# Two third products moved between u and l, and a planner's table of durations set to the trace's, in a two-layer graph kernel

## The chip, the cores and the metric

The kernel runs on one core of one Trainium2 chip. A time is that of the device for one execution, in microseconds (us); the median of several runs is compared. A profiled execution gives a trace besides. T is used below for the time since a pair of batches began on TensorE.

## The reference

The input x is 64 batches of 256 nodes with 512 features in fp32, adj is a 256 x 256 matrix of zeros and ones. Cut to what is computed:

```python
# layer 0
h = relu(layernorm(x))
q, k, v = h @ Wq.T, h @ Wk.T, h @ Wv.T
rel = adj.T * (q @ k.T)                      # per batch, 256 x 256
rel = rel / norm(rel, axis=2)
x = x + rel @ v
# layer 1
h = relu(layernorm(x))
x = x + (adj @ h) @ weight + bias
```

## The kernel before, in words

**Pairs.** Two batches (512 rows) make a pair, and 32 pairs are worked through in one program without a loop at run time; `pairs` writes them all out. Wq and Wk are multiplied once into a matrix m, so that the scores are h m h.

**Three parts.** Every fp32 operand of a matmul is split into u (rounded), l (what is left) and s (a third part that makes up for the cross terms). A product is then three: u by u, l by l, s by s, all summed in one PSUM bank. Between the second and the third, ScalarE multiplies the bank by a number near one (L340). `unit` (L328) writes this down: the matmuls of u and l, `finish`, which writes down the third product of the unit before, then the scaling. So the third product of a unit stands on TensorE after the u and l of the next one, and ScalarE has that long to scale the bank.

**Stages of a pair**, in TensorE's order: g (four units h m, read as gy), v blocks 0 and 1, scores (two units, one for each batch), gather of layer 1 for the pair before (adj times h, four units without a third product), v blocks 2 and 3, mix of the pair before (four units gather times weight, plus bias), attend (four units rel v). Attend's four results are added to x in x_ring, and layer 1's statistics and ReLU follow from them.

**Around them.** ScalarE makes the u of each split out of PSUM (L238, L247), scales banks (L340), does ReLU (L279) and the squares of the scores (L419). VectorE makes s and l (L239, L241; in the gather L248, L249), masks the scores (L415), adds results to x (L496, L555), takes the statistics of the next rows (L265 and L266, four chunks of fresh for layer 0 and four of x_ring for layer 1), and turns 32 x 32 blocks (L301 for h, L461 for the scores). Before each turning, 16 DMAs on SP's queue move the blocks to their places (L293 for h, L455 for the scores). From the turned scores come rel_u (L471, ScalarE), rel_l (L472) and rel_s_parts (L473, both VectorE), from the turned h come h_u (L316), h_l (L318) and hs (L308). SP's queue also loads the next x into fresh and into x_ring (L257), and POOL's stores results (L564).

**The order.** `Plan` (L28) takes every step with its engine, a cost in us, and the names that it reads and writes. `order` (L58) gives each step a due time, counted back from TensorE's ideal sequence, and then plays the engines forward: at each moment the engine that can start first takes, of its steps that are ready, the one that is due first (L91). A step is ready when those that it depends on are over, plus SYNC = 0.12 us if they ran on another engine (L97). The instructions are then issued in the order of these start times, engine by engine, and the scheduler leaves that order as it is. TensorE's own order is that in which the steps are written down. Where ReLU of the next h rows stands, when its block moves start and where VectorE's statistics fall is thus set by the costs in the plan.

Of the kernel before, what the change touches and what calls it, by code (L numbers as in the profile page):

```python
# [27 lines left out]
class Plan:  # L28


    SYNC = 0.12
# [26 lines left out]
    def order(self):  # L58
        ops = self.ops
        at, ideal = 0.0, {}  # L60
        for n, (engine, cost, *_) in enumerate(ops):
            if engine == "PE":
                ideal[n] = at
                at += cost
        due = [ideal.get(n, at + 50.0) for n in range(len(ops))]
        for n in range(len(ops) - 1, -1, -1):
            engine, cost, _, before, _, early = ops[n]
            due[n] -= early
            for m in before:
                e, c, _, _, late, _ = ops[m]  # L70
                due[m] = min(due[m], due[n] - c - late - (self.SYNC if e != engine else 0.0))
        left = [len(op[3]) for op in ops]
        after = [[] for _ in ops]
        for n, op in enumerate(ops):
            for m in op[3]:
                after[m].append(n)
        ready = {}
        when = [0.0] * len(ops)
        for n, k in enumerate(left):
            if not k:  # L80
                ready.setdefault(ops[n][0], []).append(n)
        free, start = {}, [0.0] * len(ops)
        for _ in ops:
            best = None
            for engine, waiting in ready.items():
                if waiting:
                    t = max(free.get(engine, 0.0), min(when[n] for n in waiting))
                    if best is None or t < best[0]:
                        best = t, engine
            t, engine = best  # L90
            n = min((n for n in ready[engine] if when[n] <= t + 0.01), key=lambda n: (due[n], n))  # L91
            ready[engine].remove(n)
            _, cost, _, _, lands, _ = ops[n]
            start[n], free[engine] = t, t + cost
            for m in after[n]:
                same = ops[m][0] == engine and not lands
                when[m] = max(when[m], t + cost + lands + (0.0 if same else self.SYNC))  # L97
                left[m] -= 1
                if not left[m]:
                    ready.setdefault(ops[m][0], []).append(m)  # L100
        self.ends = max(free.values()), at
        return [ops[n][2] for n in sorted(range(len(ops)), key=lambda n: (start[n], n))]
# [11 lines left out]
def kernel(  # L114
# [115 lines left out]
    MM, HALF = 0.231, 0.1185  # L230
# [3 lines left out]
    def split_right_ps(plan, ps, key, parts, names, at, cost=0.49):  # L234
        key = key if isinstance(key, list) else [key]
        u, l, s = ((lambda p=p: p(at)) for p in parts)
        ku, kl, ks = names
        plan.add("ACT", cost, lambda: A.activation(u(), ps, AF.Copy, scale=NEAR), key, ku)  # L238
        plan.add("DVE", 0.63, lambda: V.scalar_tensor_tensor(  # L239
            s(), f(u()), ONE, ps, op0=ALU.mult, op1=ALU.subtract), [*key, *ku], ks)  # L240
        plan.add("DVE", 0.6, lambda: V.scalar_tensor_tensor(  # L241
            l(), f(s()), -CROSS, f(u()), op0=ALU.mult, op1=ALU.add), [*ku, *ks], kl)

    def split_left_ps(plan, ps, key, parts, names, at):
        u, l, s = (p(at) for p in parts)
        ku, kl, ks = names
        plan.add("ACT", 0.49, lambda: A.activation(u, ps, AF.Copy, scale=NEAR), [key], ku)  # L247
        plan.add("DVE", 0.6, lambda: V.tensor_sub(l, ps, f(u)), [key, *ku], kl)  # L248
        plan.add("DVE", 0.6, lambda: V.scalar_tensor_tensor(  # L249
            s, f(l), CROSS + 1.0, ps, op0=ALU.mult, op1=ALU.subtract), [key, *kl], ks)  # L250
# [3 lines left out]
    def load(plan, i, src=None, name="fresh"):  # L254

        dst = fresh if name == "fresh" else ring[i % 2]
        plan.add("SP", 0.65, lambda: SP.dma_start(out=dst, in_=xs[i]), [], keys(name, TC), lands=5.5)  # L257

    def norm(plan, i, layer, src, name):

        st, mv, rs, nb = stats[layer][i % 2]
        k = f"n{layer}{i % 2}"
        for c in range(TC):
            def chunk(c=c):
                V.bn_stats(st[:, c, :], src[:, c, :])  # L265
                V.bn_aggr(mv[:, c, :], st[:, c, :])  # L266
            plan.add("DVE", 0.84, chunk, [(name, c)], [(k, c)])
        every = keys(k, TC)
        plan.add("DVE", 0.12, lambda: V.tensor_scalar(
            rs, mv[:, :, 1], 0.0, EPS, op0=ALU.max, op1=ALU.add), every, [(k, "rs")])  # L270
        plan.add("ACT", 0.2, lambda: A.activation(rs, rs, AF.Sqrt), [], [(k, "rs")])

        def end():
            V.reciprocal(rs, rs)
            V.scalar_tensor_tensor(nb, mv[:, :, 0], -1.0, rs, op0=ALU.mult, op1=ALU.mult)
        plan.add("DVE", 0.25, end, every, [(k, "rs")])

        def relu(dst, c):
            A.activation(dst, src[:, c, :], AF.Relu, bias=nb[:, c : c + 1], scale=rs[:, c : c + 1])  # L279
        return relu, [(k, "rs")]  # L280

    def h_rows(plan, i, src=fresh, name="fresh"):
        relu, needs = norm(plan, i, 0, src, name)
        for c in range(TC):
            plan.add("ACT", 0.72, lambda c=c: relu(h_rel[:, c, :], c),
                     [(name, c), *needs], [("h_rel", c)])
# [10 lines left out]
    def h_turn(plan):  # L297
        def turn(k):
            ht[k] = room(f"ht{k}", 2, T, tag=f"h_s{k}")
            for d in range(2):  # L300
                V.transpose(ht[k][:, d].rearrange("p (c n) -> p c n", c=TC), blocks[:, :, 2 * k + d])  # L301
        for k in range(2):
            plan.add("DVE", 1.16, lambda k=k: turn(k), placed_all, [("h_s", 2 * k), ("h_s", 2 * k + 1)])
# [6 lines left out]
    def h_parts(plan):  # L310
        u, l = h
        for k in range(2):
# [5 lines left out]
            plan.add("DVE", 1.14, lambda k=k, at=at: V.tensor_sub(  # L318
                l[:, at], ht[k], f(u[:, at])), [*ks, *ku], kl)
            plan.add("DVE", 1.14, lambda k=k: h_third(k), [*ku, *kl], ks)  # L320
# [7 lines left out]
    def unit(plan, first, second, drain, on=None):  # L328
# [3 lines left out]
        if on is not None:  # L332
            plan.add("ACT", 0.58, lambda: A.copy(ps, on), ["bias"], [key])
        for cost, fn, reads in first(ps):
            plan.add("PE", cost, fn, reads, [key])
# [4 lines left out]
        plan.add("ACT", 0.49, lambda: A.activation(ps, ps, AF.Copy, scale=ONE), [], [key])  # L340
# [63 lines left out]
    def scores(plan, i):  # L404
        rn = norms[i % 2]
        for b in range(NB):
# [7 lines left out]
            def drain(ps, key, b=b):  # L414
                plan.add("DVE", 0.6, lambda: V.tensor_mul(  # L415
                    rel[:, b].rearrange("p k m -> p (k m)"), ps, f(adjt[0]).rearrange("p k m -> p (k m)")),
                    [key, "adjt"], [("h_rel", b)])
                for k in range(NC):
                    plan.add("ACT", 0.53, lambda k=k: A.activation(  # L419
                        ps[:, ts(k, N)], rel[:, b, k], AF.Square, accum_out=rn[:, b, k : k + 1]),  # L420
                        [("h_rel", b)], [key, (f"rn{i % 2}", b, k)])
            unit(plan, first, second, drain)

    def turn_scores(plan, i, by_pe=False):
# [3 lines left out]
        plan.add("DVE", 0.12, lambda: V.reciprocal(rn, rn), [], sums)  # L428
        if by_pe:
            u, l = (part.rearrange("p b t k n -> p b (t k n)") for part in rel_p)  # L430
            for b in range(NB):
# [11 lines left out]
                plan.add("ACT", 0.49, lambda ps=ps, b=b: A.activation(  # L443
                    u[:, b], ps, AF.Copy, scale=NEAR), [key], [("rel_u", b)])
                plan.add("DVE", 0.63, lambda ps=ps, b=b: V.tensor_sub(
                    l[:, b], ps, f(u[:, b])), [key, ("rel_u", b)], [("rel_l", b)])
                plan.add("DVE", 0.6, third, [("rel_u", b), ("rel_l", b)],
# [11 lines left out]
        for b in range(NB):  # L459
            for k in range(NC):  # L460
                plan.add("DVE", 0.33, lambda b=b, k=k: V.transpose(  # L461
# [10 lines left out]
        plan.add("DVE", 1.14, lambda: V.tensor_sub(l, flat_raw(), f(u)), [*halves, *rel_u], rel_l)  # L472
        plan.add("DVE", 1.14, lambda: V.scalar_tensor_tensor(  # L473
            whole(rel_third()), f(l), CROSS, f(u), op0=ALU.mult, op1=ALU.subtract), [*rel_u, *rel_l], halves)

    def attend(plan, i, exact):
        slot, rn = i % 2, norms[i % 2]
        for c in range(TC):
# [16 lines left out]
            def drain(ps, key, b=b, n=n, c=c):  # L495
                plan.add("DVE", 0.63, lambda: V.scalar_tensor_tensor(  # L496
# [4 lines left out]
            unit(plan, first, second, drain)  # L501

    def layer_1(plan, i, exact):
        slot = i % 2
        relu, needs = norm(plan, i, 1, ring[slot], f"x{slot}")
        for c in range(TC):
            x_c = [(f"x{slot}", c), *needs]
            if not exact:
                plan.add("ACT", 0.72, lambda c=c: relu(changing("late", "h2", 8, D)[:, c], c), x_c,
# [4 lines left out]
            plan.add("ACT", 0.72, lambda c=c: relu(raw()[:, c % 2], c), x_c,  # L514
                     [("raw", 0), ("raw", 1)] if not c else k)
            plan.add("ACT", 0.53, lambda c=c, u=u: A.copy(late(u), raw()[:, c % 2]), k, [("late", u)])
            plan.add("DVE", 0.6, lambda c=c, u=u, l=l: V.tensor_sub(
# [28 lines left out]
    def mix(plan, i, blocks_of=range(4)):  # L546
        slot = i % 2
        for c in blocks_of:
# [5 lines left out]
            def drain(ps, key, c=c):  # L554
                plan.add("DVE", 0.6, lambda: V.tensor_add(  # L555
# [63 lines left out]
    adjt = []  # L619
# [4 lines left out]
    def first_turn(plan):  # L624

        u, l = h
        for d in range(DC):
# [6 lines left out]
            plan.add("ACT", 0.49, lambda ps=ps, d=d: A.activation(  # L634
                u[:, d], ps, AF.Copy, scale=NEAR), [key], [("h_u", d)])
            plan.add("DVE", 0.63, lambda ps=ps, d=d: V.tensor_sub(
                l[:, d], ps, f(u[:, d])), [key, ("h_u", d)], [("h_l", d)])
        for k in range(2):
            kept = [(f"h_{q}", d) for q in "ul" for d in (2 * k, 2 * k + 1)]
            plan.add("DVE", 1.14, lambda k=k: h_third(k), kept, [("h_s", 2 * k), ("h_s", 2 * k + 1)])  # L640
# [7 lines left out]
    def first_g(plan):  # L648

        banks = [next_bank() for _ in range(DC)]  # L650
        for k in range(3):
            for e, (ps, key) in enumerate(banks):
# [3 lines left out]
                if k == 2:  # L656
                    plan.add("ACT", 0.49, lambda ps=ps: A.activation(ps, ps, AF.Copy, scale=ONE), [], [key])
# [21 lines left out]
    def pairs(exact):  # L679
# [6 lines left out]
        plan.add("ACT", 0.49, lambda: A.copy(adjt[0].rearrange("p m n -> p (m n)"), bank[6]), [("bank", 6)], ["adjt"])  # L686
# [83 lines left out]
```

## Time and profile before

| | |
|---|---|
| median of 3 runs | 1571.62 us (1569.84 to 1572.21) |
| profiled execution | 1571.74 us |
| its span, first to last instruction | 1569.96 us |
| VectorE busy | 1357.6 us, 86% |
| ScalarE busy | 1023.8 us, 65% |
| scaling of banks, L340 | 572 times, 583 ns each |
| load of fresh, issue to landing | 5.9 us |
| load of x_ring, issue to landing | 7.9 us |
| row moves of h (L293), 64 KB each | 496, 2.1 us to landing |
| block moves of the scores (L455), 32 KB each | 464, 1.9 us to landing |

The page gives busy times with the tail of each instruction; on VectorE an operation of 128 x 512 is listed with some 0.68 us, and the next starts 0.60 us after it. A matmul of 512 columns is listed with 389 ns, while four of them start within 0.907 us, since they overlap. PEld is the load of a weight, which runs ahead of its matmul. In a list of waits, the engine to the left of the arrow waited for the one to the right; in a timeline the wait stands in brackets behind the instruction that it delayed. SPq is SP's queue of DMA issues.

### The profile page before, as it was taken

What the parts mean: (1) busy time and instruction counts of PE and PEld (TensorE: products, weight loads), DVE (VectorE), ACT (ScalarE), POOL (GpSimd) and SP (SyncE); (2) the same over time, 40 slices, a digit from 0 to 9 for tenths busy, and PEclk for the clock granted to TensorE, in tenths of its full rate; (3) what the DMA queues carried; (4) which work ended last, traced back from release to release, by engine and by line L of the source; (5) the groups of instructions that cost most, each with busy time, mean ns of one, the idle gap of its engine ahead of it and who ended that gap; (6) DMA issues with size and microseconds to landing.
All of it is one profiled execution on the core that took longest, in us unless ns stands there. A gap on an engine that the chain in (4) does not pass through costs nothing.

```text
span 1570.0 us, 22385 instructions
## 1 busy us (share of the span) xinstructions
PE 1557.2 (99%) x8046; PEld 1322.8 (84%) x8046; DVE 1357.6 (86%) x2419; ACT 1023.8 (65%) x1941; POOL 24.3 (2%) x39
## 2 busy tenths in 40 slices
PE   9999999999999999999999999999999999999998
PEld 6788888888888888888888888888888888888886
DVE  6997889898888988898888889888989888988786
ACT  5567666676667676666666676766666766767654
POOL 0000000000000000000000000000000000000000
PEclk9999999999999999999999999999999999999999
DMA  6431444324444334443244442344433344433311
GB/s 195 113 81 41 118 111 120 69 77 111 115 115 93 82 81 120 110 119 68 77 112 114 114 112 67 81 118 111 118 75 85 97 119 110 121 67 79 84 54 56
DMA packets 433127, 153.62 MB, mean 98 GB/s; under 512 B 389872, under 2 KB 390128, under 8 KB 433008
## 3 DMA queue, kind: packets, MB, share of 16 engines
q1 hardware_dynamic: 422784, 116.46, 31.5%
q0 software_dynamic: 8432, 32.51, 5.6%
q10 hardware_dynamic: 1792, 3.15, 0.5%
q8 instruction: 65, 1.06, 0.3%
q14 instruction: 54, 0.44, 0.1%
HBM read 70.78 MB, written 33.55 MB: 66 GB/s over the span
## 4 chain that ended last, share of the span: by engine, by line
PE 83%; SPq 5%; DVE 5%; DMA 4%; ACT 2%; issue 1%; ACTq 0%; DVEq 0%
PE bank L228 83%; SPq L293 4%; DMA fresh<-in_x_dram 2%; SPq L455 2%; ACT h_rel L279 1%; DVE st L265 1%; DMA bias_bc<-in_L_gnn_bias_dram 1%; DMA x_ring<-in_x_dram 1%; DMA h_rel<-h_rel 0%; DVE gy_s L239 0%; DVE gy_l L241 0%; ACT bank L340 0%; DVE h_rel L415 0%; DVE late_parts L239 0%; DVE mv L266 0%
## 5 line engine op out<-in xcount | busy, mean ns | idle before, releaser
L340 ACT ACTIVATE bank<-bank 128x512 f32<-128x512 f32 x572 | 333.4, 583 | 321.5 <-PE bank L228 318.3
L228 PE MATMUL bank<-wv_s,hs 128*128 128x512 f32 x512 | 139.9, 395 | 0.2
L228 PE MATMUL bank<-w_u,gy_u 128*128 128x512 f32 x512 | 137.9, 391 | 0.0
L228 PE MATMUL bank<-wv_u,h_u 128*128 128x512 f32 x512 | 137.6, 390 | 0.0
L228 PE MATMUL bank<-w_s,gy_s 128*128 128x512 f32 x512 | 137.5, 391 | 0.0
L228 PE MATMUL bank<-w_l,gy_l 128*128 128x512 f32 x512 | 137.3, 390 | 0.0
L228 PE MATMUL bank<-wv_l,h_l 128*128 128x512 f32 x512 | 136.9, 389 | 0.0
L228 PE MATMUL bank<-h_u,m_u 128*128 128x512 f32 x512 | 136.5, 389 | 0.3 <-DVE m_s L239 0.3
L228 PE MATMUL bank<-h_l,m_l 128*128 128x512 f32 x512 | 136.6, 389 | 0.1
L228 PE MATMUL bank<-hs,m_s 128*128 128x512 f32 x512 | 136.3, 389 | 0.0
L239 DVE SCALAR_TENSOR_TENSOR gy_s<-gy_u,bank 128x512 fp32r<-128x512 f32 x128 | 86.2, 676 | 43.3 <-ACT gy_u L238 43.3
L228 PEld LDWEIGHTS bank<-w_u,gy_u 128*128 128x128 f32 x512 | 96.0, 188 | 20.8
L228 PEld LDWEIGHTS bank<-w_s,gy_s 128*128 128x128 f32 x512 | 95.7, 188 | 21.2 <-ACT bank L340 1.2
L228 PEld LDWEIGHTS bank<-w_l,gy_l 128*128 128x128 f32 x512 | 96.1, 188 | 20.7
L228 PEld LDWEIGHTS bank<-h_u,m_u 128*128 128x128 f32 x512 | 96.0, 188 | 20.5 <-ACT wv_u L238 0.5
L228 PEld LDWEIGHTS bank<-h_l,m_l 128*128 128x128 f32 x512 | 96.0, 188 | 20.4 <-DVE h_l L318 0.5
L228 PEld LDWEIGHTS bank<-wv_l,h_l 128*128 128x128 f32 x512 | 96.1, 188 | 20.2
L228 PEld LDWEIGHTS bank<-hs,m_s 128*128 128x128 f32 x512 | 96.1, 188 | 19.9
L228 PE MATMUL bank<-adjt_r,late_parts 128*128 128x256 f32 x896 | 112.8, 277 | 0.0
L228 PEld LDWEIGHTS bank<-wv_s,hs 128*128 128x128 f32 x512 | 92.8, 188 | 22.8 <-ACT bank L340 5.2
L228 PEld LDWEIGHTS bank<-wv_u,h_u 128*128 128x128 f32 x512 | 93.7, 188 | 17.8
L228 PEld LDWEIGHTS bank<-adjt_r,late_parts 128*128 128x128 f32 x896 | 107.5, 188 | 0.0
(110 smaller groups left out, 3078.3 us busy)
## 6 DMA issues: line engine op xcount, KB each, us to landing
fresh<-in_x_dram SPq DMA_DIRECT2D x31, 1024.0 KB, 5.9
blocks<-h_rel SPq DMA_DIRECT2D x496, 64.0 KB, 2.1
x_ring<-in_x_dram SPq DMA_DIRECT2D x31, 1024.0 KB, 7.9
out_dram<-x_ring POOLq DMA_DIRECT2D x31, 1024.0 KB, 5.3
h_rel<-h_rel SPq DMA_DIRECT2D x464, 32.0 KB, 1.9
blocks<-in_L_gnn_Wv_dram ACTq DMA_DIRECT2D x1, 1024.0 KB, 10.9
x_ring<-in_L_gnn_weight_dram SPq DMA_DIRECT2D x1, 1024.0 KB, 12.4
out_dram<-x_ring SPq DMA_DIRECT2D x4, 256.0 KB, 2.3
```

Source lines behind the costliest of these rows:

```text
L228: nc.tensor.matmul(out, left, right, start=first, stop=True, skip_group_check=True)
L239: plan.add("DVE", 0.63, lambda: V.scalar_tensor_tensor(s(), f(u()), ONE, ps, op0=ALU.mult, op1=ALU.subtract), [*key, *ku], ks)
L265: V.bn_stats(st[:, c, :], src[:, c, :])
L279: A.activation(dst, src[:, c, :], AF.Relu, bias=nb[:, c : c + 1], scale=rs[:, c : c + 1])
L293: plan.add("SP", 0.65, lambda j=j, k=k: SP.dma_start(out=blocks[ts(j, S), :, :, ts(k, S)], in_=hv[ts(k, S), :, :, ts(j, S)]), keys("h_rel" ...
L340: plan.add("ACT", 0.49, lambda: A.activation(ps, ps, AF.Copy, scale=ONE), [], [key])
L455: plan.add("SP", 0.65, lambda j=j, k=k: SP.dma_start(out=pv[ts(j, S), :, ts(k, S)], in_=rv[ts(k, S), :, ts(j, S)]), [("h_rel", 0), ("h_rel ...
```

## The change

It has two parts, and adds or removes no instruction.

First, `unit` gets a parameter `behind`: the number of the step of u and l ahead of which the waiting third product is written down. Two places use it. In scores, batch 0, the third product of v block 1 comes after the u matmuls and ahead of the l matmuls. In attend, block 0, the third product of the unit before (mix block 3) comes between u and l. All other units keep their order.

Second, the plan's costs are set to durations of the trace, each changed by some hundredths of a us (the largest: the turning of h, L301, from 1.16 to 1.24, ReLU from 0.72 to 0.76, L274 and L275 together from 0.25 to 0.37, the landing of fresh from 5.5 to 6.0 and of x_ring from 5.5 to 8.0), and a step on VectorE that depends on another one on VectorE is ready only CHAIN = 0.11 us after it, where it was ready at once.

The diff, cut to its core (the other changed lines only change a cost in the same way):

```diff
-    SYNC = 0.12
+    SYNC, CHAIN = 0.12, 0.11
...
-                when[m] = max(when[m], t + cost + lands + (0.0 if same else self.SYNC))
+                when[m] = max(when[m], t + cost + lands + (self.CHAIN * (engine == "DVE") if same else self.SYNC))
...
-    MM, HALF = 0.231, 0.1185
+    MM, HALF = 0.229, 0.1165
...
-        plan.add("DVE", 0.63, lambda: V.scalar_tensor_tensor(
+        plan.add("DVE", 0.61, lambda: V.scalar_tensor_tensor(
             s(), f(u()), ONE, ps, op0=ALU.mult, op1=ALU.subtract), [*key, *ku], ks)
...
-        plan.add("SP", 0.65, lambda: SP.dma_start(out=dst, in_=xs[i]), [], keys(name, TC), lands=5.5)
+        plan.add("SP", 0.65, lambda: SP.dma_start(out=dst, in_=xs[i]), [], keys(name, TC), lands=6.0 if name == "fresh" else 8.0)
...
-            plan.add("DVE", 0.84, chunk, [(name, c)], [(k, c)])
+            plan.add("DVE", 0.82, chunk, [(name, c)], [(k, c)])
...
-        plan.add("DVE", 0.25, end, every, [(k, "rs")])
+        plan.add("DVE", 0.37, end, every, [(k, "rs")])
...
-            plan.add("DVE", 1.16, lambda k=k: turn(k), placed_all, [("h_s", 2 * k), ("h_s", 2 * k + 1)])
+            plan.add("DVE", 1.24, lambda k=k: turn(k), placed_all, [("h_s", 2 * k), ("h_s", 2 * k + 1)])
...
-    def unit(plan, first, second, drain, on=None):
+    def unit(plan, first, second, drain, on=None, behind=9):
...
-        for cost, fn, reads in first(ps):
+        for n, (cost, fn, reads) in enumerate(first(ps)):
+            if n == behind:
+                finish(plan)
             plan.add("PE", cost, fn, reads, [key])
         finish(plan)
...
-            unit(plan, first, second, drain)
+            unit(plan, first, second, drain, behind=9 if b else 2)
...
-            unit(plan, first, second, drain)
+            unit(plan, first, second, drain, behind=9 if c else 1)
```

## The prediction

> **What bounds the kernel now.** I read the page's busy shares first, then the waits of all engines, then the chain that ended last, then the timelines of two pairs of batches.
>
> ```profile
> PE 1557.2 (99%) x8046; PEld 1322.8 (84%) x8046; DVE 1357.6 (86%) x2419; ACT 1023.8 (65%) x1941; POOL 24.3 (2%) x39
> ```
>
> TensorE is busy 99% of the span, with no order of work that could shorten its matmuls; only its gaps can be won or lost. I took the start of the first h_u,m_u matmul of each pair from the timeline of TensorE and subtracted neighbours. Thirteen of the pairs 2 to 30 take 47.54 us (two of them 47.55), the rest up to 48.61. So 47.54 is the floor of a pair, and the excess over it, summed over these 29 pairs, is 6.95 us. That sum, about 3 us at the start (pairs 0 and 1) and 1.3 us in pair 31 are all there is to win by reordering.
>
> The chain that ended last says where the excess comes from:
>
> ```profile
> 737.50 1.35 SPq L293
> 738.90 1.76 SPq L293
> 741.39 1.39 SPq L293
> 744.17 5.73 DMA fresh<-in_x_dram
> ...
> 801.60 721.01 PE bank L228 x3766
> ```
>
> Row moves of h (L293), then the load of fresh behind them, and then a stall; after 801.6 us TensorE alone is the chain. The timelines of VectorE and TensorE show such a stall:
>
> ```profile
> 798.54 0.69 DVE L265 BATCH_NORM_STATS2 st<-fresh 128x6 f32<-128x512 f32 x1 [0.72 <-DMA fresh<-in_x_dram]
> 800.16 0.65 DVE L239 SCALAR_TENSOR_TENSOR gy_s<-gy_u,bank 128x512 fp32r<-128x512 f32 x1
> 800.85 0.69 DVE L241 SCALAR_TENSOR_TENSOR gy_l<-gy_s,gy_u 128x512 fp32r<-128x512 f32 x1
> 801.60 0.50 PE L228 MATMUL bank<-h_l,gy_l 128*128 128x256 f32 x2 [0.34 <-DVE gy_l L241]
> ```
>
> The statistics of fresh stand in VectorE's queue ahead of the last gy_l. When the load is late, gy_l is late, and TensorE waits. The waits list this load 19 times, 13.8 us. The shifted ScalarE work behind it explains the later small waits on the bank scaling of L340.
>
> **What the Trainium skill says.** "TensorE: Matmul & The Clock Gate", Back-to-back issue gap, gives N/2.4 + 2.5 ns, 216 ns for N = 512; here four matmuls start 0.907 us apart, 227 ns each, so the floor is near it. "VectorE: DVE Perf Modes", The DRAIN you can't avoid, says a semaphore between chained operations costs nothing extra. The trace differs, and decides: L239 to L241, which depends on it, starts 0.71 us later, independent neighbours 0.60. The change's new delay of 0.11 is thus true of this trace. "DMA: Bandwidth & Descriptors", Anatomy of one DMA, puts some 2.0 us of fixed cost on a DMA; the 32 KB moves of L455 land after 1.9.
>
> **The change, part by part.** Times below are T, counted from the start of a pair; the floor pair that begins at 1308.89 us gives them. Its lines:
>
> ```profile
> 1332.53 0.69 DVE L415 TENSOR_TENSOR h_rel<-bank,adjt_r 128x512 f32<-128x512 f32 x1 [1.25 <-PE bank L228]
> ...
> 1347.69 1.20 DVE L318 TENSOR_TENSOR h_l<-ht,h_u 128x1024 fp32r<-128x1024 f32 x1
> 1348.81 1.21 DVE L472 TENSOR_TENSOR rel_l<-rel_s_raw,rel_u 128x1024 fp32r<-128x1024 f32 x1
> 1350.06 1.23 DVE L473 SCALAR_TENSOR_TENSOR rel_s_parts<-rel_l,rel_u 128x1024 fp32r<-128x1024 f32 x1
> 1351.20 1.22 DVE L318 TENSOR_TENSOR h_l<-ht,h_u 128x1024 fp32r<-128x1024 f32 x1
> ```
>
> ```profile
> 1350.97 0.39 PE L228 MATMUL bank<-v_low,rel_l 128*128 128x512 f32 x1
> 1351.20 0.39 PE L228 MATMUL bank<-late_parts,rel_l 128*128 128x512 f32 x1
> 1351.43 1.08 PE L228 MATMUL bank<-w_s,gy_s 128*128 128x512 f32 x4
> 1353.25 0.39 PE L228 MATMUL bank<-v_low,rel_s_parts 128*128 128x512 f32 x1
> ```
>
> *The moved third products.* No instruction is added. In scores, four wv_s matmuls (0.91 us) go ahead of h_l,gy_l; in attend, four w_s matmuls go ahead of the first rel_l. So gy_l is due 0.91 us later, and rel_l at T = 42.08 + 0.91 = 42.99. The scaling of the moved bank (L340, 0.58 us) loses that much cover: for mix block 3 its product now starts at 42.09; its last matmul ends at 40.88, and 0.04 + 0.58 + 0.05 later it is scaled, 41.55. Cover 0.5 us: nothing lost. Attend block 0 is worse: its last rel_l matmul would start at 43.22 and end 0.39 later; scaling ends at 44.23, plus 0.05. Its third product is due at 44.37. A late weight load costs more than its lateness: a matmul whose load had to wait keeps the next one off for 0.335 us instead of 0.227, so I add 0.108. 44.28 + 0.108 - 44.37 = 0.02 us. Nothing, so long as ScalarE is free; the built order puts no other ScalarE work between those scalings any more.
>
> *The new order.* Listing the instructions of both kernels engine by engine, I find that VectorE's order changes in every pair. The statistics of fresh leave the place ahead of gy_l: three of four chunks now stand among the gathers' splits, and ReLU, row moves and the load of fresh follow 10 us later than before. ReLU ends about T = 8.5 or 9.4; sixteen moves took 10.8 us where no output store ran (pairs 0 and 1), 12.2 to 14.1 otherwise; the store is over at about T = 6 now, so I take 10.8; 5.9 us of landing gives T = 25.2 or 26.1. The first statistics come at 27.7 or 28.6. The wait on fresh is gone, and with it the waits on gy_l and their wake: I credit 6.3 of the 6.95 us, and leave 0.65 for waits on L455 (pairs 2, 22, 23).
>
> *What it costs.* Three chunks at 0.81 us are 2.44 us put between the second L415 (T = 23.64) and L473. Before, VectorE idled there: 0.3 us ahead of L248, 0.7 after L428, 0.3 ahead of L301. And the delay of 0.11 lets the planner fill it: L473 depends on L472, isn't ready when L472 ends, and another ready operation of 0.58 or 1.14 us is put between. From pair 2 two orders alternate, 14 times each.
> Even pairs: L415 at 23.64, first L248 at 24.25; then fourteen operations at 0.60 (8.4), three chunks (2.44), four L301 (2.45), four L461 (1.31), L555 0.58, L318 1.13, L428 0.1, one dependent step 0.11: L472 at 40.75. L318 follows, then L473 at 43.02; it takes 1.23, release 0.05, load 0.108: 44.41 against 44.37, 0.04 us of wait.
> Odd pairs: the first L248 comes ahead of the second L415, at 23.27; the same sum with 0.6 for L415, 0.27 us of wait for ScalarE (L238) and both L318 ahead gives L472 at 41.69. rel_l is good at 43.06 against 42.99 (0.07). L555 is next, and L473 at 43.41 gives 44.80 against 44.44: 0.36. Together 0.43 us.
> 14 x 0.04 + 14 x 0.43 = 6.6 us. Each start may be off by 0.2 us, so 2 to 13 us; I take 6.6.
>
> *Start and end.* At the start the four chunks of fresh go into VectorE's idle time, seen here:
>
> ```profile
> 21.65 0.69 DVE L636 TENSOR_TENSOR h_l<-bank,h_u 128x512 fp32r<-128x512 f32 x1 [3.46 <-ACT h_u L634]
> ```
>
> The h_l behind are done 1.6 us sooner, but L274 still waits for ScalarE's root at 24.9, so the first L239 of m starts at 25.4, not 25.99: 0.6 us won. In pair 0 rel_l follows w_l without L274, L275 and L428 ahead: 0.5 us. In pair 31, 0.2. Pair 1 I count at nothing.
>
> *The sum.* The profiled execution took 1571.74 us (span 1569.96), 0.12 above the median of 1571.62. 1571.74 + 6.6 - 6.3 - 0.6 - 0.5 - 0.2 = 1570.7 us: no change that counts.
>
> **Rivals.** *The chain is on time* (1564.1): all credits, no new wait. L473 need only start 0.04 us sooner in even and 0.43 in odd pairs. For it: the ends of the matmuls are modelled, and 0.108 may not apply. Against: VectorE runs without a gap from L248 on, at spacings that repeat to 0.01 us between floor pairs.
> *The load of fresh is late again*, slower: if sixteen moves keep taking 13.3 us, the load lands at 9.4 + 13.3 + 5.9 = 28.6, and odd pairs want it at 27.7; 0.9 us x 14 = 12.6 more, 1583.3. It decides from 11.9 us of moves on. Against it: the store no longer runs beside them. For it: the loads now share the DMA engines with L455.
> *VectorE's chain is later than I count*, 0.25 us in all 28 pairs: 1577.7.
> That nothing is reordered is ruled out by the listing.
>
> **How the numbers follow.** Forecast 0.42, on time 0.29, late load 0.20, later chain 0.09. About 0.2% (3.1 us) is what a measurement of this kernel can tell from no change. On time is nearly all faster, and the low side of the forecast adds some: 0.34. The late load, the later chain and a little of the forecast are slower: 0.30. Same 0.36. The range, 1563.5 to 1581, leaves out the low end of the first rival and the high end of the late load.
>
> **What would show it.** Pair starts: even pairs 47.6, odd 48.0, hardly any spread. VectorE's wait on fresh near 0. Waits of TensorE on rel_s_parts (L473), none on gy_l. If L265 waits on fresh at T = 28, or TensorE's floor changes, I am wrong.

## The result and the profile after

The changed kernel takes 1575.01 us (median; 1573.49 to 1576.78), the kernel before, beside it on the same chip, 1571.65 us (1569.84 to 1574.32): a ratio of 1.0020, 95% interval 1.0014 to 1.0026. It is slower by 0.2%, where I had expected 1570.7 us. The profiled execution took 1576.78 us, with a span of 1574.35 us, 4.4 us more than before. It is the slowest of the 22, 1.8 us above their median, so a part of the loss in its trace belongs to this execution alone. Numbers of lines from L343 on are those of before plus 3: L415 is now L418, L455 is L458, L472 is L475, L473 is L476.

Cut by the start of each pair on TensorE, as in the prediction, the two spans differ like this (us):

| | before | after | difference | predicted |
|---|---|---|---|---|
| up to the start of pair 0 | 26.81 | 26.40 | -0.4 | -0.6 |
| pair 0 | 36.89 | 35.86 | -1.0 | -0.5 |
| pair 1 | 49.75 | 48.94 | -0.8 | 0 |
| pairs 2 to 30, above 29 x 47.54 | 6.94 | 14.57 | +7.6 | +0.3 |
| pair 31 and the end | 70.90 | 69.93 | -1.0 | -0.2 |

The loss is all in the steady pairs. Two lines of the page answer to those of before, the busy times and the chain that ended last:

```profile
PE 1557.1 (99%) x8046; PEld 1318.6 (84%) x8046; DVE 1331.0 (85%) x2419; ACT 1024.9 (65%) x1941; POOL 24.3 (2%) x39
...
PE 72%; DVE 14%; SPq 7%; ACT 2%; DMA 2%; issue 1%; DVEq 0%; ACTq 0%
```

TensorE does the same work, and VectorE is less busy than before (1331.0 us for 1357.6), but it now lies on the chain with 14% of the span, for 5% before. The waits of all engines tell which of its operations are late (engine and line, the releaser; us in total, times, the longest):

```profile
PEld bank L228 <- ACT bank L343: 17.6, 38, 1.6
DVE h_rel L418 <- DMA blocks<-h_rel: 11.6, 5, 2.5
...
PEld bank L228 <- DVE rel_l L475: 6.2, 15, 0.9
...
PE bank L228 <- DVE rel_s_parts L476: 2.9, 15, 0.5
DVE st L265 <- DMA fresh<-in_x_dram: 2.3, 1, 2.3
...
DVE rel_s_raw L464 <- DMA h_rel<-h_rel: 1.9, 3, 1.0
```

The wait on fresh, 13.8 us in 19 places before, is down to one of 2.3, and TensorE waits on gy_l no more. In their place stand rel_l and rel_s_parts, 15 times each, about once in each odd pair, as predicted. Of the first line, 8.5 us before, 14.1 us are the weight load of the first rel_s_parts product, once in each pair: with the moved products it follows close on the scaling of its bank. TensorE itself waits 1.1 us in all on the scaling. (In odd pairs the line names the wrong engine: in pair 13 the scaling is over at T = 44.25, and that load starts at 44.67, as rel_s_parts is done.) New, and in no part of my sum, is the second line: the masking of the scores (L418), which writes into h_rel, waits for the row moves of h, which read h_rel.

An undisturbed odd pair (pair 13, from 639.08) shows the predicted wait. First VectorE, then TensorE (start, duration; the wait in brackets):

```profile
678.46 2.32 DVE L318 TENSOR_TENSOR h_l<-ht,h_u 128x1024 fp32r<-128x1024 f32 x2
680.69 1.22 DVE L475 TENSOR_TENSOR rel_l<-rel_s_raw,rel_u 128x1024 fp32r<-128x1024 f32 x1
681.82 0.68 DVE L558 TENSOR_TENSOR x_ring<-bank,x_ring 128x512 f32<-128x512 f32 x1
682.43 1.22 DVE L476 SCALAR_TENSOR_TENSOR rel_s_parts<-rel_l,rel_u 128x1024 fp32r<-128x1024 f32 x1
```

```profile
683.23 0.39 PE L228 MATMUL bank<-late_parts,rel_l 128*128 128x512 f32 x1
683.79 0.47 PE L228 MATMUL bank<-v_low,rel_s_parts 128*128 128x512 f32 x1 [0.17 <-DVE rel_s_parts L476]
```

L558 stands between L475 and L476. L476 starts at T = 43.35 (predicted 43.41), and the matmul that reads it starts 0.56 us after its neighbour, not 0.23. Such pairs take 47.98 us; undisturbed even pairs 47.57. That is 0.44 and 0.03 above 47.54, 14 of each: 6.6 us, as in the sum. But in 16 of the 29 pairs there is more: eight odd pairs (3, 5, 7, 17, 19, 21, 25, 27) are together 4.3 us above 47.98, and the even ones 3.7 us above 47.57. These 8.0 us are what the experiments had to explain.

### The profile page after: what moved, and what is told of

The parts are those of the page before. It is cut to its first block, busy times and chain, and to the rows that moved or that the text cites. A ratio compares the mean times of both kernels' runs of the same rounds, so it can differ in the third digit from the quotient of the medians.

```text
span 1574.4 us, 22399 instructions
## 1 busy us (share of the span) xinstructions
PE 1557.1 (99%) x8046; PEld 1318.6 (84%) x8046; DVE 1331.0 (85%) x2419; ACT 1024.9 (65%) x1941; POOL 24.3 (2%) x39
## 4 chain that ended last, share of the span: by engine, by line
PE 72%; DVE 14%; SPq 7%; ACT 2%; DMA 2%; issue 1%; DVEq 0%; ACTq 0%
PE bank L228 72%; SPq L458 5%; DVE h_l L318 2%; SPq L293 2%; DVE rel_s_raw L464 1%; DVE x_ring L558 1%; DVE rel_s_parts L476 1%; DVE rel_l L475 1%; DVE ht L301 1%; DMA h_rel<-h_rel 1%; DVE late_parts L241 1%; DVE gy_s L249 1%; DVE late_parts L239 1%; DVE gy_l L248 1%; DVE st L265 1%
## 5 line engine op out<-in xcount | busy, mean ns | idle before, releaser
L343 ACT ACTIVATE bank<-bank 128x512 f32<-128x512 f32 x572 | 333.3, 583 | 371.1 <-PE bank L228 369.9
L418 DVE TENSOR_TENSOR h_rel<-bank,adjt_r 128x512 f32<-128x512 f32 x64 | 44.1, 689 | 95.0 <-PE bank L228 65.4
L228 PEld LDWEIGHTS bank<-w_u,gy_u 128*128 128x128 f32 x512 | 96.0, 188 | 20.8
L228 PEld LDWEIGHTS bank<-wv_l,h_l 128*128 128x128 f32 x512 | 96.1, 188 | 20.1
```

The source lines that it names most:

```text
L228: nc.tensor.matmul(out, left, right, start=first, stop=True, skip_group_check=True)
L343: plan.add("ACT", 0.5, lambda: A.activation(ps, ps, AF.Copy, scale=ONE), [], [key])
L418: plan.add("DVE", 0.605, lambda: V.tensor_mul(rel[:, b].rearrange("p k m -> p (k m)"), ps, f(adjt[0]).rearrange("p k m -> p (k m)")), [key ...
```

## The experiments

All were run in five rounds beside the kernel before; ratios are to that one, since the same kernel before had medians from 1572.07 to 1575.33 us in these jobs. "Excess" is the sum of pairs 2 to 30 above 29 x 47.54 us in the profiled execution. That is one execution of each kernel: those of the changed kernel and of experiment 4 were the slowest of their kernels' runs, that of experiment 5 was the fastest, so differences of 1 to 2 us between two excesses show little. The recorded expectations call the runs by names: e2_costs is experiment 2 here, e3_nochain 3, e6_ahead 7, e9_e3pool 9 and e13 or e13_chainonly 11.

**1. Moved products alone.** The kernel before with the new `unit` and nothing else:

```diff
+            if n == behind:
+                finish(plan)
```

> The kernel before with the moved third products alone (all costs as before, no delay). VectorE and ScalarE keep the order of before, only TensorE's order changes. Theory (the move is harmless or helps, the new order of VectorE is what costs): the 1.8 us of waits on gy_l go, the bank scalings of attend block 0 cost 0.02 us a pair; 1569.5 us, 0.1 to 0.2% under before. Rival (the moved third product takes the cover of its bank scaling and is itself the loss): a wait on the scaling of 0.2 us or more in every attend, 1577 us or more.

Measured 1574.67 us, ratio 1.0007 (0.9999 to 1.0016): no change that this measurement can tell, with an excess of 10.25 us. Neither number came true. Undisturbed pairs are at 47.57. Where the moves of the scores land late, as in pair 22, the moved product has lost the cover that it had. Here is that pair on ScalarE and TensorE in the kernel before, and then with the moved products:

```profile
1112.48 0.58 ACT L340 ACTIVATE bank<-bank 128x512 f32<-128x512 f32 x1
...
1113.15 1.14 PE L228 MATMUL bank<-w_s,gy_s 128*128 128x512 f32 x4
```

```profile
1111.35 1.04 ACT L473 ACTIVATE rel_u<-rel_s_raw 128x1024 fp32r<-128x1024 f32 x1
1112.30 1.51 ACT L279 ACTIVATE h_rel<-fresh,nb,rs 128x512 f32<-128x512 f32 x2
1113.71 0.57 ACT L342 ACTIVATE bank<-bank 128x512 f32<-128x512 f32 x1
...
1114.33 1.18 PE L228 MATMUL bank<-w_s,gy_s 128*128 128x512 f32 x4 [0.63 <-ACT bank L342]
```

ScalarE does rel_u and two ReLU ahead of the bank's scaling, all delayed by those moves. Before, the scaled bank was ready (1113.06) as its product's turn came (1113.15). Now the turn comes 0.91 us sooner, and TensorE waits 0.63. The pair is 48.48 us instead of 47.61.

**2. The new model alone.** The changed kernel with the third products at their old places:

```diff
-            unit(plan, first, second, drain, behind=9 if b else 2)
+            unit(plan, first, second, drain)
...
-            unit(plan, first, second, drain, behind=9 if c else 1)
+            unit(plan, first, second, drain)
```

> The changed kernel with its costs and its delay, but with no third product moved. Theory (rel_l and rel_s_parts late on VectorE): rel_l is due 0.91 us earlier than in the changed kernel, so odd pairs wait 0.98 us for rel_l where they wait 0.43 in all now; 14 x 0.55 = 7.7 us more than the changed kernel, some 1583 us. Rival (the moved products are the loss): at or under the kernel before, 1570 us.

Measured 1583.63 us, ratio 1.0063 (1.0050 to 1.0077), as the theory had it. Undisturbed odd pairs take 48.47 us, even ones 47.54. So the model's order costs 0.93 us in an odd pair, of which the moved products take back 0.49 by making rel_l due later. The two parts of the change are not a sum: alone the products bring nothing, with the new order 0.4%.

**3. Without the delay.**

```diff
-    SYNC, CHAIN = 0.12, 0.11
+    SYNC, CHAIN = 0.12, 0.0
```

> The changed kernel with CHAIN = 0: moved products and costs of the trace, but no delay between dependent VectorE steps. The built order has no statistics of fresh among the gathers' splits, rel_s_parts stands right behind rel_l, and the row moves are early again as in the kernel before. Theory (the delay brought the bad order): no wait on rel_s_parts, waits on fresh shorter than before; 1568 us. Rival (the durations brought it): as the changed kernel, 1575 us.

Measured 1571.8 us, ratio 0.9986 (0.9980 to 0.9993): faster than both kernels. Its order is again that of the kernel before round rel_l, ReLU and row moves lie round the start of the pair, all pairs have a floor of 47.61, and the wait on fresh is back (14.3 us). So without the delay the slowdown is gone.

**4. rel_l and rel_s_parts as one step**, so that nothing can be put between them:

```diff
-        plan.add("DVE", 1.135, lambda: V.tensor_sub(l, flat_raw(), f(u)), [*halves, *rel_u], rel_l)
-        plan.add("DVE", 1.135, lambda: V.scalar_tensor_tensor(
-            whole(rel_third()), f(l), CROSS, f(u), op0=ALU.mult, op1=ALU.subtract), [*rel_u, *rel_l], halves)
+        def both():
+            V.tensor_sub(l, flat_raw(), f(u))
+            V.scalar_tensor_tensor(
+                whole(rel_third()), f(l), CROSS, f(u), op0=ALU.mult, op1=ALU.subtract)
+        plan.add("DVE", 2.38, both, [*rel_u], [*rel_l, *halves])
```

> The changed kernel with rel_l and rel_s_parts written down as one step of the plan (2.38 us on VectorE), so that nothing stands between them; nothing else is edited. Theory (the filler between them is the steady loss): odd pairs keep 0.07 us of wait on rel_l, 0.36 on rel_s_parts goes, even pairs lose their 0.03; 14 x 0.39 = 5.5 us less than the changed kernel, 1569.5 us. Rival (the loss is in the disturbed pairs, whose row moves or loads are late): no more than 1 us less, 1574 us.

Measured 1577.04 us, ratio 1.0016 (1.0008 to 1.0024), a miss. What it was made for did come: undisturbed pairs take 47.60 in both parities, so the 0.44 us of an odd pair were the operation between the two. But the order of even pairs changed too. The first chunk of fresh is now the second operation after the masking instead of the eighth, and the load isn't there:

```profile
DVE st L265 <- DMA fresh<-in_x_dram: 16.5, 15, 2.9
```

The even pairs' excess went from 4.11 to 10.45 us, more than the odd ones gained (10.46 to 6.93). (The medians of the two kernels do not differ clearly.) This is the prediction's rival of the late load, by another door: the moves are no slower, but the statistics are asked for sooner.

**5. Scores in a tile of their own.** The order on TensorE, VectorE and ScalarE stays that of the changed kernel; only the write after read on h_rel goes. (Lines are one higher.)

```diff
-    wq_last, wk_last = room("wq_last", D), room("wk_last", D)
+    rel_own = room("rel_own", T * NC)
+    wq_last, wk_last = rel_own[:, :D], rel_own[:, D:]
...
-    rel = flat_rel[:, : T * NC].rearrange("p (b k m) -> p b k m", b=NB, k=NC)
+    rel = rel_own.rearrange("p (b k m) -> p b k m", b=NB, k=NC)
```

> The changed kernel in its own order, but the masked scores get a tile of their own instead of the first half of h_rel (the room comes from two weight tiles that only the start uses). So L418 no longer has to wait until the sixteen row moves have read h_rel. Theory: this write-after-read is what delays the disturbed odd pairs (3, 5, 7, 17, 19, 21, 25, 27: together 4.3 us above the 47.98 of the clean ones). It goes: odd pairs all near 48.0, no wait of L418 on the moves, ratio to the kernel before 0.9995 (1.0021 less 4.3 of 1575). Clean even and odd pairs stay at 47.57 and 47.98. Rival: something else makes the disturbed pairs late (the moves themselves, or the loads beside them), and the ratio stays at 1.002.

Measured 1575.81 us, ratio 1.0006 (0.9998 to 1.0014), between the two theories. Pair 21 in the changed kernel, SyncE's queue and VectorE, and then the same pair with the own tile:

```profile
1031.72 11.55 SPq L293 DMA_DIRECT2D blocks<-h_rel  x16
...
1045.28 0.69 DVE L418 TENSOR_TENSOR h_rel<-bank,adjt_r 128x512 f32<-128x512 f32 x1 [2.98 <-PE bank L228]
```

```profile
1031.93 11.16 SPq L294 DMA_DIRECT2D blocks<-h_rel  x16
...
1044.47 0.69 DVE L419 TENSOR_TENSOR rel_own<-bank,adjt_r 128x512 f32<-128x512 f32 x1 [1.96 <-PE bank L229]
```

In the first, the last of sixteen moves is issued at T = 20.15 and lands 2.1 us later, at T = 22.26; L418 starts at T = 22.79 instead of the 21.76 of undisturbed pairs. In each pair of the changed kernel in which L418 is late, it starts 0.2 to 0.5 us after the last landing. The brackets name TensorE in both, although it was long done in the first: the instruction waits for several things. In the second the moves are late too (the last lands at T = 21.85), and L419 starts at T = 21.77, in this pair and in every other from pair 2 on, also where the last move lands at T = 23.06 (pair 27). So the lateness of L418 is the write after read, and with it go seven of the eight odd pairs, 4.1 of the 4.3 us; in pair 17 L418 is only 0.33 us late, and the moves of the scores are late too. But the odd pairs as a whole gained nothing: their excess is 10.80 us for 10.46, since each now pays a new wait:

```profile
DVE ht L302 <- DMA h_rel<-rel_own: 2.1, 11, 0.2
```

The wait on the moves has gone over to their next reader, the turning of h, which had needed none as long as L418 ahead of it had waited. There it costs 0.27 us: L302 starts at T = 34.16 in 13 of the 14 odd pairs, instead of 33.89 in undisturbed ones, though the row moves are over by T = 23.1. The list names the moves of the scores, which L302 does not read; they signal on the same semaphores. Its start does not follow their landings, so I put the 0.27 us down to the wait itself, which no run tests. In the even pairs an operation of 0.57 us stands right ahead, and L302 starts at T = 34.00 in both kernels. All odd pairs now take 48.27 to 48.37 but for pair 3. What the trace gains in its pairs, it gains in the even ones (excess 2.68 us for 4.11, 0.9 of it in pair 26). The ratios differ by 0.14%, some 2.2 us; with some 4 us of new waits (14 x 0.29) beside it, I estimate that the write after read was worth about 6 us.

**6. Early row moves in the new order.**

```diff
-    def h_place(plan, early=8.0):
+    def h_place(plan, early=14.0):
```

> The changed kernel with the row moves due 14 us ahead of their need in the planner instead of 8: ReLU and moves come at the start of the pair again, no chunk of fresh lies among the splits of the gathers, the load of fresh is again issued behind sixteen early moves. Theory: the loss of the changed kernel comes from the late ReLU and moves, not from the moved products or the model's durations as such. Clean pairs 47.57 in both parities (as its pair 30 shows, which has this order), no wait of L418 on the moves, but the wait on fresh is back at some 14 us, of which about 6 reach TensorE as in the kernel before; ratio 0.9995 to 1.0. Rival: the delay between VectorE operations has spoiled the order elsewhere too, and the ratio stays at 1.002.

Measured 1576.95 us, ratio 1.0016 (1.0008 to 1.0024): the rival's number, by another way. From pair 5 on the theory holds: both parities are at 47.57, and 26 pairs are together 4.3 us above that. But pairs 2, 3 and 4 take 49.28, 52.41 and 50.47 us, 9.5 us more than 47.57 each. Their moves start at T = 3.3 to 4.8, where from pair 5 on they start 5.1 us ahead of the pair; the load stands behind them, and the statistics wait for it up to 5.8 us. It takes this order three pairs to get back into step.

**7. A planner that looks ahead.**

```diff
-            n = min((n for n in ready[engine] if when[n] <= t + 0.01), key=lambda n: (due[n], n))
+            n = min((n for n in ready[engine] if when[n] <= t + 0.12), key=lambda n: (due[n], n))
+            t = max(t, when[n])
```

> The changed kernel with a planner that, at each choice, also takes an operation that becomes ready within 0.12 us if it is due earlier, so that the delay of 0.11 between dependent VectorE operations no longer calls for another operation in between. Theory: the delay is in the durations rightly, and it does harm only because the greedy planner fills each gap of 0.11 with an operation of 0.4 to 0.8 us; with this the order is nearly that without the delay, and so is the time: ratio 0.9985. Rival: the harm comes from the longer due times or from the other durations, and the ratio stays near 1.002.

Measured 1566.44 us, ratio 0.9950 (0.9936 to 0.9964): the fastest beside 8, ahead of both kernels, and better than expected. rel_s_parts follows rel_l again, undisturbed pairs take 47.57, the excess is 5.38 us. The wait on fresh is still there:

```profile
DVE st L266 <- DMA fresh<-in_x_dram: 12.2, 17, 1.4
```

But now most of it is covered. By the trace, the planner has put the masking of the first scores between the two steps of the statistics' end (L269 and L274 of before), where it stood behind both, and so behind ScalarE's root too. No run tests that step alone.

**8. Looking ahead without the delay** (3 and 7 together).

> The changed kernel without the delay (as e3_nochain), but with the planner that looks 0.12 us ahead (as e6_ahead). Theory: without the delay there is no gap of 0.11 to be filled, so looking ahead gives next to nothing here: ratio near that of e3_nochain (0.9986), and the delay with the look ahead (0.995) is better than no delay. Rival: looking ahead is a gain by itself, whatever the delay: ratio 0.995.

Measured 1564.65 us, ratio 0.9956 (0.9943 to 0.9970). My theory for this falls: looking ahead gains by itself, whatever the delay; the two intervals overlap. So experiment 7 does not show that a model with the true delay is worth anything, only that looking ahead undoes its harm. The plan also has SYNC = 0.12 us between engines, and looking ahead covers that too; whether its gain comes from there was not tested.

**9. The load of fresh on GpSimd's queue**, in experiment 3's kernel:

```diff
+        E, q = ("POOL", G) if name == "fresh" else ("SP", SP)
-        plan.add("SP", 0.65, lambda: SP.dma_start(out=dst, in_=xs[i]), [], keys(name, TC), lands=6.0 if name == "fresh" else 8.0)
+        plan.add(E, 0.8 if name == "fresh" else 0.65, lambda: q.dma_start(out=dst, in_=xs[i]), [], keys(name, TC), lands=6.0 if name == "fresh" else 8.0)
```

> The changed kernel without the delay (as e3_nochain), and with the load of fresh issued by GpSimd's queue, so that it is not behind the sixteen row moves on SyncE. Theory: what is left above the clean pairs in the kernel before and in e3_nochain (some 7 us) is the load of fresh that is issued only after 10.8 us of moves. It then starts as soon as the ReLU has read fresh, the wait of the statistics on it (14.3 us in e3_nochain) goes below 3, and the ratio is 0.9945. Rival: the load shares the transfer engines with the moves, or waits behind the store on GpSimd's queue, and what it gains is lost on the moves: ratio 0.9985 as without it.

Measured 1570.82 us, ratio 0.9974 (0.9964 to 0.9984). The wait on fresh fell from 14.3 us to one of 2.2 at the start, and the excess from 9.33 to 6.05 us. Of the 0.41% that I expected over experiment 3, 0.12 came, and the two intervals overlap. The trace shows two reasons. Pairs 13 to 16 and 18 to 20 are still 0.28 to 0.85 us above 47.61; in pair 13 the turning of the scores (L465) starts 0.7 us late and TensorE waits 0.58 us on the scaling, as in experiment 1. And the time from TensorE's last matmul to the end is 7.8 us instead of 5.8.

**10. Both, 7 and 9.**

> The planner of e6_ahead and the load of fresh on GpSimd's queue as in e9_e3pool. Theory: the two gains are of different waits, so they add: the clean pairs stay at 47.57, the wait of the statistics on fresh goes from 12.2 us to below 3, and of it some 3 us had reached TensorE: ratio 0.9935 (e6_ahead has 0.995). Rival: in e6_ahead the wait on fresh was hidden already, and the pairs that are left above the clean ones (12 to 20, in e9_e3pool too) wait for the row moves of the scores: ratio 0.995 as without it.

Measured 1567.93 us, ratio 0.9973 (0.9963 to 0.9983), not better than 7 but rather worse (the intervals just touch). The rival was right that the wait on fresh was covered already: the excess is 5.56 us with it and 5.38 without. The rest is at both ends: pair 0 starts 0.8 us later, and the end takes 8.3 us instead of 6.2.

**11. The delay alone** in the kernel before:

```diff
-                when[m] = max(when[m], t + cost + lands + (0.0 if same else self.SYNC))
+                when[m] = max(when[m], t + cost + lands + (0.11 * (engine == "DVE") if same else self.SYNC))
```

> The kernel before with the delay of 0.11 between dependent VectorE operations in its model, and nothing else of the change. Its built order has ReLU and moves at the start of the pair as before, but two steps of h's low parts ahead of rel_l and the drain of x between rel_l and rel_s_parts. Theory: the delay by itself already brings the worse order round rel_l, and without the moved products that costs as in pair 30 of e2_costs, which has the same steps there: 0.25 us in each of 29 pairs, 7.3 us, ratio 1.0046. Rival: the delay harms only with the other durations, which push the ReLU to the middle of the pair: ratio 1.000.

Measured 1618.04 us, ratio 1.0290 (1.0276 to 1.0304), far off both. The waits say why:

```profile
DVE st L265 <- DMA fresh<-in_x_dram: 60.5, 31, 3.6
PEld bank L228 <- DVE gy_l L241: 31.5, 26, 2.1
PE bank L228 <- DVE gy_l L241: 26.3, 25, 1.9
```

The gaps of 0.11 us are now filled with the chunks of fresh, between the splits that TensorE waits for, and ahead of the landing.

**12. The same order with the load on GpSimd's queue** (the planner still counts it on SyncE's):

```diff
-        plan.add("SP", 0.65, lambda: SP.dma_start(out=dst, in_=xs[i]), [], keys(name, TC), lands=5.5)
+        plan.add("SP", 0.65, lambda: (G if name == "fresh" else SP).dma_start(out=dst, in_=xs[i]), [], keys(name, TC), lands=5.5)
```

> e13_chainonly (the kernel before with the delay alone, 1.029) in the same order on TensorE, VectorE and ScalarE, but the load of fresh is issued on GpSimd's queue, so it no longer stands behind sixteen row moves on SyncE. Theory: the 2.9% of e13 are the load: its order asks for the four chunks of fresh between the splits of the gathers, before the load can be there (60.5 us of waits of the statistics on fresh, and then 57.8 us of TensorE on gy_l). With the load early these waits go below 5 and 10 us, the pairs fall to 47.8, where the waits on rel_l leave them, and the ratio is 1.005. Rival: TensorE's waits on gy_l come from the delay's order itself, and the ratio stays above 1.02.

Measured 1580.27 us, ratio 1.0034 (1.0021 to 1.0048), as the theory had it: undisturbed pairs take 47.79 us, and the waits are

```profile
PEld bank L228 <- DVE rel_l L472: 18.3, 29, 1.4
...
DVE st L265 <- DMA fresh<-in_x_dram: 4.0, 6, 1.3
...
PEld bank L228 <- DVE gy_l L241: 0.6, 1, 0.6
```

So of the 2.9% of the delay alone, 2.6 are the load behind sixteen moves. In the rest are the waits on rel_l: 0.25 us in each pair.

## Why the prediction was wrong

**The floor and the new waits held.** 47.57 and 47.98 in undisturbed pairs, 6.6 us as in the sum; the operation between rel_l and rel_s_parts is the cause of the odd part (experiment 4). The 0.02 us of the moved product is 0.03. The wait on fresh went, and with it gy_l. The 216 ns of "TensorE: Matmul & The Clock Gate", Back-to-back issue gap, in the Trainium skill are no support for the floor: that section gives them for a matmul by itself, and some 131 ns for a stream. The trace decides: 227 ns between matmuls of 512 columns, before and after.

**The credit failed**: "I credit 6.3 of the 6.95 us, and leave 0.65 for waits on L455". The excess that is not the new waits was 8.0 us, not 0.65, and the sign "hardly any spread" failed in 16 pairs. Two things were missing.

*A reader of h_rel.* I saw ReLU and the sixteen moves go later, and asked whether the load behind them would be late. I did not ask what the moves themselves hold. They read h_rel, L415 writes the scores there, and it starts only after they have landed. The numbers were at hand: ReLU was to end at T = 8.5 or 9.4; the 10.8 us of moves run to the end of the last issue, which starts 10.2 us after the first; and the table of before has 2.1 us to landing. That makes 20.8 or 21.7, and the first L415 of a floor pair started at T = 21.7. From pair 3 on, the last move before was issued at T = 6.4 to 8.4, so the cover had been over 11 us; in an undisturbed odd pair it became 0.4. There the last move is issued at T = 19.3 to 19.7 and lands just in time; in five of the eight others the issues stretch to T = 20.1 to 20.8, and in pairs 7 and 27 the last move takes 3.7 and 3.6 us to land. Experiment 5 takes this lateness away: 4.1 us in the odd pairs, and in pair 26, where L418 started at T = 22.93 too and which takes 47.61 us there instead of 48.53, 0.9 more. It also shows that in the odd pairs another wait takes as much.

*Waits that were hidden.* I took nearly all of the old excess for the load of fresh. But in seven pairs of the kernel before (2, 15, 17 to 19, 22 and 23) the second masking is on time and the moves of the scores land late; they hold 2.0 of the 6.9 us, not 0.65. With the load out of the way, 6.05 us of excess stay (experiment 9), 4.0 of them above its own floor of 47.61; that kernel has the moved products, so these are not the same waits, and no run takes the load alone out of the kernel before. In pair 22 of the kernel before, rel_u starts 0.83 us late, and the pair takes 47.61, because rel_l had cover. In the changed kernel rel_u (L474) of that pair starts 1.1 us late and the pair takes 48.64: no cover is left, and each delay counts in full. Of the 8.0 us, L418 accounts for 5.0 (seven odd pairs and pair 26), and pairs 2, 16, 17, 18 and 22, in which the moves of the scores land late, for 2.6. This second part is read from the trace; no run here removes it.

**Smaller terms.** Start, pairs 0 and 1 and the end gave 3.2 us, not 1.3, which by luck hid a part of the miss. The sum is then +6.6 from the new waits, 8.0 of disturbances in place of 6.9, and -3.2: the +4.4 us of span, but for rounding. The medians differ by 3.4.

**The rivals.** The chain was not on time, since both new waits came. It was not later than counted either: L475 starts at T = 40.61 and 41.61, for 40.75 and 41.69. The late load did not come true in the changed kernel (one wait of 2.3 us), but it makes experiment 11 slow, as 12 shows, and by their traces 4 and 6 too. The sentence "The change's new delay of 0.11 is thus true of this trace" stands, and is no reason to put it into this planner: a duration that is right makes a greedy order worse where it opens a gap too short for anything, and something of 0.6 us is put in. Which of the other durations pushes ReLU to the middle of the pair stays open: with the delay alone it stays at the start (experiment 11), and without the delay too (experiment 3).

## What to carry to other kernels

When a step is moved later, list what it reads as well as what it makes: whoever overwrites its inputs now has less cover, and here the writer started 0.2 to 0.5 us after the last of the moves that read its tile had landed. Work out the cover of every such pair before and after; here 11 us became 0.4, and no wait of the profile before pointed to this pair. It did list the same kind of wait at another place, ReLU that writes h_rel behind the moves of the scores:

```profile
ACT h_rel L279 <- DMA h_rel<-h_rel: 12.0, 18, 1.6
```

An excess that a profile puts down to one wait is not won by removing that wait, if others are hidden behind it or the new order leaves them no slack. And where a greedy planner is told a truer latency, let it look ahead by that latency: this took the changed kernel from a ratio of 1.0020 to 0.9950. It gains without the latency as well (0.9986 to 0.9956, experiments 3 and 8); in the kernel before, by itself, it was not tried.

## What the runs showed of the hardware

- With a wait on sixteen moves ahead of it that were over for 11 us and more, L302 started 0.27 us later in 13 of 14 odd pairs (experiment 5); in even pairs, behind an operation of 0.57 us, it started no later. That the wait itself is the cause was not tested.
- Sixteen moves of 64 KB took 10.0 to 10.1 us from the first to the last issue where nothing disturbed them, up to 11.6 elsewhere, and landed in 2.1 us, the slowest in 4.2 (the changed kernel).
- With the load of fresh on GpSimd's queue, it lands in 7.7 us instead of 6.0 (experiments 9 and 3) or 6.1 (10 and 7), and in 10.2 instead of 6.0 in experiments 12 and 11. The time from the last matmul to the end grows from 5.8 to 6.2 us to 7.8 to 8.3 us in all three kernels that do it. What is waited for there the traces don't name.
